# GpSimd's sums for the product M, the attention dots, and layer 3's statistics: three moves in a four-layer graph kernel on one core

## The chip, the core and the metric

The kernel runs on one core of a Trainium2 chip. Five engines of the core work side by side: TensorE (PE; its weight loads are shown as PEld) multiplies matrices into PSUM, VectorE (DVE), ScalarE (ACT) and GpSimd (POOL) work element by element, and SyncE (SP) starts transfers. Each engine takes its instructions strictly in the order in which the program emits them, and waits on semaphores for the others. The metric is the device time of one execution in microseconds (us); lower is better.

## The reference

x is 128 x 128 x 512 (batch, nodes, features), adj is 128 x 128, all float32. Four layers follow one another, and each ends in a normalization over the 512 features:

```python
x = layernorm(x + ((adj @ x) @ W0 + bias0))
q, k, v = x @ Wq.T, x @ Wk.T, x @ Wv.T
rel = adj.T * (q @ k.T);  rel = rel / norm(rel, axis=2)
x = layernorm(x + rel @ v)
h = x @ W;  e = leaky_relu(h@a1[:, None] + h@a2[None, :]) * adj
x = layernorm(x + elu(softmax(e) @ h + beta * h))
A = adj @ x;  C = A + b
x = layernorm(x + max(relu(A + (C - A)), over the last axis))
```

In layer 3 the sum A + (C - A) has the largest element of a row of A, plus b: a row gets relu(max(A row) + b) added to every element.

## The kernel before

The 128 batch elements are worked in 32 groups of four (G = 4). A group passes the four layers; several groups are in flight at once.

**Products.** Four products of a group use a seven-multiplication scheme for 2 x 2 blocks (names y, m, v, z; PSUM tiles r_y, r_m, r_v, r_z). Their left factors need four sums of blocks, which GpSimd builds (`left_factors`, lines 294 to 311: s_y, s_x, s_z; the sums for M and V are the s_x made by `x_sums`). A product has seven steps in the order 1, 2, 6, 5, 7, 3, 4; each step's result is taken from PSUM by ScalarE (a copy) or VectorE (an addition) 0.72 after the step (`product`, lines 339 to 362). Steps 1, 6, 7 and 4 share one PSUM region, so step 7's result must have been taken before step 4 begins, and y's step 6 needs step 1's taken. M's step 6 needs the second sum, step 5 the first, step 7 the third, step 3 the fourth.

**Order.** Nothing is ordered by a planner at run time. Every piece of work is given a time in slots (`TABLE`, lines 231 to 246; 28 slots a group, about 2.4 us each), all pieces are sorted by it and emitted in that order (line 783), which fixes each engine's queue. `FIRST` and `LAST` hold other times for the first two and the last three groups; in `LAST` they are in us, divided by 2.48. The times within a group run over 108 slots, so group g+1's `m` at 28 stands at g's slot 56, and next to it on the queues are g's dots, g+2's `bias` and `y_sums` and g-1's `elu`.

**Around the change.** In layer 1, `residual` (lines 545 to 556) adds rel @ v out of PSUM (p_o) and takes statistics (BATCH_NORM_STATS2 into st, the aggregate into mv). `dots` (lines 559 to 572) multiplies a row block of x2 with two vectors on VectorE and accumulates (tile scr; two per batch element, both inputs in SBUF); `scale_dots` (lines 574 to 587) turns the sums d into layer 2's s1 and s2 in three tiny operations; `spread` transposes them (p_s). `norm` (lines 375 to 406) makes 1/sqrt(variance) with a GpSimd power (ve into rstd), then nmean on VectorE and one ScalarE ACTIVATE per batch element. `elu` (lines 716 to 724) has two VectorE operations with both inputs in SBUF (x from c, x from m). `biased` (line 429) adds bias0 on GpSimd once p_y has been read from x. Layer 3 (lines 747 to 771): `widen` computes adj @ x into p_a, `top` takes the row maximum (mx), adds b and clips (top, VectorE), and ScalarE adds top to x; then statistics and `norm` as in the other layers.

Of the kernel before, what the change touches and what calls it, by code (L numbers as in the profile page):

```python
# [8 lines left out]
FP = mybir.dt.float32  # L9
AF = mybir.ActivationFunctionType  # L10
ALU = mybir.AluOpType
AX = mybir.AxisListType

EPS = 1e-5
# [15 lines left out]
def kernel(  # L30
# [33 lines left out]
    pe, dve, act, pool = (InOrder(tc, e) for e in (nc.tensor, nc.vector, nc.scalar, nc.gpsimd))  # L64
    sync = InOrder(tc, nc.sync)
    B, N, D = x.shape
    P = 128
# [4 lines left out]
    G = 4  # L72
# [5 lines left out]
    work = ctx.enter_context(tc.tile_pool(name="work", bufs=1))  # L78
    small = ctx.enter_context(tc.tile_pool(name="small", bufs=4))
    psum = ctx.enter_context(tc.tile_pool(name="psum", bufs=4, space=bass.MemoryType.PSUM))  # L80

    def bank(name):
        return psum.tile([P, D], FP, tag="ps", name=name)
# [8 lines left out]
    x1, x2, x3 = {}, {}, {}  # L92
# [28 lines left out]
    b3_sb = const.tile([P, 1], FP)  # L121
# [4 lines left out]
    mhalf = const.tile([P, G], FP)  # L126
# [93 lines left out]
    def emit(at, f, *args):  # L220
        pieces.append((at, lambda: f(*args)))

    def each(at, f):
        for b in range(len(at)):
            emit(at[b], f, b)

    def row(at, step, n=G):
        return [at + i * step for i in range(n)]


    TABLE = dict(
        load=[-20], y=row(0.5, 1), bias=row(1.3, 1), y_sums=row(5.2, 0.5), y_w=row(7, 1, 7),
        stats0=row(14.4, 0.4), norm0=[16.2], apply0=row(16.8, 0.33),
        turn=row(21.4, 1), turn_blocks=row(18.4, 0.6),
        move=row(20.5, 0.1), x_sums=row(25.3, 0.5), m=row(28, 1, 7), scores=row(36.5, 1),
        masked=[39.95], squares=[40.4], turn_rel=[40.3],
        move_rel=row(41.2, 0.1), inverse=[42.5], v=row(42, 1, 7), attend=row(50.6, 1),
        residual=row(51.0, 1), dots=row(54.2, 1.1), norm1=[55.2], scale=[58.8],
        apply1=row(65.4, 0.33),
        spread=[61.6], leaky=[62.0], weighted=[63.4], greatest=[64.3], exps=[64.4],  # L240
        divide=[65.8], turn_att=[68.6], with_beta=[69.0], gather=row(71.5, 1),
# [2 lines left out]
        widen=[98.7, 100.0, 103.6, 104.6], top=[99.1, 100.4, 104.0, 105.0],  # L244
        stats3=[99.8, 101.1, 104.7, 105.7], norm3=[106.2], apply3=row(107, 0.33), store=[108.5],
# [8 lines left out]
            stats3=[27.0, 29.9, 32.2, 35.8], norm3=[42.0], apply3=row(44.0, 0.8), store=[47.4],  # L254
        ),
        NG - 2: dict(
            scale=[5.6], apply1=row(24.3, 0.8), spread=[6.9], leaky=[7.4], weighted=[9.0],
# [4 lines left out]
            top=[73.7, 74.6, 78.0, 78.9], stats3=row(79.8, 0.9), norm3=[83.4],  # L262
            apply3=row(84.8, 0.8), store=[88.2],
        ),
        NG - 1: dict(
            m=[0.0, 1.73, 3.46, 5.2, 7.4, 9.1, 10.8], scores=row(12.7, 0.9), masked=[16.4],
            squares=[17.2], turn_rel=[17.1], move_rel=row(18.0, 0.1), inverse=[20.0], v=[16.7, 18.4, 21.0, 22.7, 25.3, 27.9, 30.5],
            attend=row(33.2, 0.86), residual=row(34.1, 1.65), norm1=[40.65], dots=row(40.7, 1.53),
            scale=[47.0], apply1=row(47.5, 0.8), spread=[48.9], leaky=[49.4], weighted=[51.0],
# [5 lines left out]
            top=[83.5, 84.4, 85.3, 87.0], stats3=[86.1, 87.9, 88.8, 89.7],  # L275
            norm3=[86.9, 88.7, 89.6, 90.5], apply3=[88.3, 90.1, 91.0, 91.9],
# [91 lines left out]
    def stats(s, g, b, t):  # L368
        if b == 0:
            s["mv"] = small.tile([P, G, 2], FP, tag="mv", name=f"mv_{g}", bufs=6)  # L370
        st = small.tile([P, 6], FP, tag="st", name=f"st_{g}_{b}")
        dve.bn_stats(st, t)
        dve.bn_aggr(s["mv"][:, b, :], st)

    def norm(at, apply_at, s, g, t):

        n = G // len(at)

        def spread(i):
            sl = slice(i * n, i * n + n)  # L380
            ve = small.tile([P, n], FP, tag=f"ve{n}", name=f"ve_{g}_{i}")
            dve.tensor_scalar(ve, s["mv"][:, sl, 1], EPS, None, op0=ALU.add)
            s["r", i] = small.tile([P, n], FP, tag=f"rstd{n}", name=f"rstd_{g}_{i}")
            pool.tensor_tensor(s["r", i], ve, mhalf[:, sl], ALU.pow)

        def shift(i):
            sl = slice(i * n, i * n + n)
            s["nm", i] = small.tile([P, n], FP, tag=f"nmean{n}", name=f"nmean_{g}_{i}")
            dve.scalar_tensor_tensor(
                s["nm", i], s["mv"][:, sl, 0], -1.0, s["r", i], op0=ALU.mult, op1=ALU.mult  # L390
            )

        def apply(b):
            i, j = b // n, b % n
            act.activation(
                t()[:, b, :],
                t()[:, b, :],
                AF.Identity,
                bias=s["nm", i][:, j : j + 1],
                scale=s["r", i][:, j : j + 1],  # L400
            )

        each(at, spread)
        for i in range(len(at)):
            emit(apply_at[i * n] - 0.1, shift, i)
        each(apply_at, apply)
# [340 lines left out]
    def layer3(g, t):  # L747
        s = {}

        def widen(b):  # L750
            s["a", b] = bank(f"p_a_{g}_{b}")
            pe.matmul(s["a", b], adjT, x3[g][:, b, :], start=True, stop=True)

        def top(b):
            x = x3[g][:, b, :]
            mx = small.tile([P, 1], FP, tag="mx", name=f"mx_{g}_{b}")
            dve.tensor_reduce(mx, s["a", b], AX.X, ALU.max)
            tp = small.tile([P, 1], FP, tag="top", name=f"top_{g}_{b}")
            dve.tensor_scalar(tp, mx, b3_sb, 0.0, op0=ALU.add, op1=ALU.max)
            act.activation(x, x, AF.Identity, bias=tp)  # L760

        def store(i):
            for b in range(i * n, i * n + n):
                sync.dma_start(out[g * G + b], x3[g][:, b, :])

        n = G // len(t["store"])
        each(t["widen"], widen)
        each(t["top"], top)
        each(t["stats3"], lambda b: stats(s, f"3_{g}", b, x3[g][:, b, :]))
        norm(t["norm3"], t["apply3"], s, f"3_{g}", lambda: x3[g])  # L770
        each(t["store"], store)


# [6 lines left out]
    for g in range(NG):  # L780
        for layer in (layer0, layer1, layer2, layer3):
            layer(g, times(g))
# [31 lines left out]
```

## Time and profile before

| | |
|---|---|
| time, median of three | 2234.3 us (2232.62 to 2236.04) |
| span of the profiled execution | 2234.4 us |
| TensorE, weight loads | 2182.9 us busy (98%), 1842.1 us (82%) |
| VectorE, ScalarE, GpSimd | 1794.9 us (80%), 980.0 us (44%), 983.1 us (44%) |
| dots (scr from x and wa), 256 of them | 286.2 us, 1169 ns each |
| statistics, 512 | 352.1 us, 688 ns each; aggregates 93.3 us |
| sums for M (s_x), 128 | 195.1 us |
| Relu-like top on VectorE, 128 | 27.5 us, 215 ns each |

The profile is one execution. A group line has the engine, the operation, output and inputs by the program's names (numbers left out), and how often it ran. The timeline has start and length in us, engine, line, operation, tiles, shapes, and in brackets how long the engine had stood idle and for whom. Line 26 is the helper through which every instruction goes, so groups are told apart by their tiles.

### The profile page before, as it was taken

How to read it: one execution, taken by the hardware profiler on the slowest of the kernel's cores; microseconds unless marked ns; L12 is line 12 of the kernel's file. 1: busy time of each engine (PE TensorE's matmuls, PEld its weight loads, DVE VectorE, ACT ScalarE, POOL GpSimd, SP SyncE). 2: the span in 40 equal slices, each digit the busy share in tenths (PEclk: the TensorE clock that was granted, in tenths of full speed). 3: DMA queues.
4: the chain of work that ended last, by engine and by line, in shares of the span. 5: the costliest groups of instructions: out<-in, count | busy, mean ns of one | idle time of the engine just before them, and what ended most of it. 6: DMA issues, size and time to landing. Idle time of an engine off the chain costs nothing.

```text
span 2234.4 us, 31661 instructions
## 1 busy us (share of the span) xinstructions
PE 2182.9 (98%) x11073; PEld 1842.1 (82%) x11073; DVE 1794.9 (80%) x3534; ACT 980.0 (44%) x1936; POOL 983.1 (44%) x743
## 2 busy tenths in 40 slices
PE   7999999999999999999999999999999999999996
PEld 5888888888888888888888888888888888888873
DVE  4668888778878788888788888788888788887788
ACT  2224444444444454444444444444344444444535
POOL 3435454435455344544344554344553354443322
PEclk9999999999999999999999999999999999999998
DMA  4010222211222211222201222202222112221101
GB/s 166 25 32 19 60 57 62 62 28 40 60 59 62 62 19 48 59 60 62 59 19 52 58 61 62 52 22 55 57 62 63 41 28 59 58 62 43 21 28 57
DMA packets 333294, 115.15 MB, mean 52 GB/s; under 512 B 297424, under 2 KB 297552, under 8 KB 333136
## 3 DMA queue, kind: packets, MB, share of 16 engines
q1 hardware_dynamic: 331936, 110.77, 19.6%
q10 hardware_dynamic: 1200, 2.36, 0.3%
q8 instruction: 89, 1.46, 0.3%
q14 instruction: 69, 0.57, 0.1%
HBM read 39.65 MB, written 33.55 MB: 33 GB/s over the span
## 4 chain that ended last, share of the span: by engine, by line
PE 75%; DVE 20%; issue 3%; POOL 1%; ACT 1%; DMA 0%; DVEq 0%; ACTq 0%; POOLq 0%
PE r_v L26 17%; PE r_y L26 15%; PE r_z L26 14%; PE r_m L26 8%; DVE scr L26 6%; DVE x L26 6%; PE p_z L26 5%; PE p_o L26 5%; PE p_a L26 5%; PE p_rel L26 4%; DVE st L26 2%; PE p_y L26 2%; DVE tT L26 1%; DVE d L26 1%; PE p_m L26 1%
## 5 line engine op out<-in xcount | busy, mean ns | idle before, releaser
L26 ACT ACTIVATE x<-x,nmean,rstd 128x512 f32<-128x512 f32 x512 | 385.8, 808 | 187.5 <-DVE nmean L26 187.4
L26 DVE BATCH_NORM_STATS2 st<-x 128x6 f32<-128x512 f32 x512 | 352.1, 688 | 56.7 <-ACT x L26 47.9
L26 DVE SCALAR_TENSOR_TENSOR scr<-x,wa 128x512 f32<-128x512 f32 x256 | 286.2, 1169 | 0.0
L26 POOL TENSOR_TENSOR rstd<-ve,mhalf 128x4 f32<-128x4 f32 (+1 forms) x134 | 145.2, 1083 | 286.9 <-DVE ve L26 280.7
L26 POOL TENSOR_TENSOR x<-x,bias_sb 128x512 f32<-128x512 f32 x128 | 193.2, 1519 | 76.9 <-PE p_y L26 76.4
L26 POOL TENSOR_TENSOR s_x<-xT 128x512 f32<-128x512 f32 x64 | 95.8, 1497 | 256.5 <-DMA xT<-xB 237.6
L26 ACT ACTIVATE x<-x,top 128x512 f32<-128x512 f32 x128 | 92.4, 722 | 229.1 <-DVE top L26 228.8
L26 DVE TENSOR_TENSOR x<-r_y,x 128x512 f32<-128x512 f32 x224 | 151.4, 676 | 27.1 <-PE r_y L26 27.0
L26 ACT COPY c<-r_z 128x512 f32<-128x512 f32 x124 | 71.8, 579 | 221.5 <-PE r_z L26 221.5
L26 ACT COPY yT<-p_y 128x512 f32<-128x512 f32 x128 | 75.1, 587 | 206.5 <-PE p_y L26 206.5
L26 PEld LDWEIGHTS p_y<-adjT,x 128*128 128x128 f32 x1024 | 135.8, 195 | 13.1 <-ACT adjT L26 5.2
L26 DVE SCALAR_TENSOR_TENSOR x<-p_o,rn,x 128x512 f32<-128x512 f32 x128 | 95.9, 749 | 59.9 <-PE p_o L26 56.0
L26 PE MATMUL p_y<-adjT,x 128*128 128x128 f32 x1024 | 136.7, 278 | 6.4 <-ACT adjT L26 4.9
L26 PEld LDWEIGHTS p_z<-eT,x 128*128 128x128 f32 x1024 | 133.9, 192 | 8.4 <-DVE x L26 1.2
L26 DVE SCALAR_TENSOR_TENSOR x<-m,x 128x512 f32<-128x512 f32 x128 | 129.7, 1013 | 13.6 <-DVE x L26 0.9
L26 PEld LDWEIGHTS p_rel<-xT,tT 128*128 128x128 f32 x1024 | 134.1, 191 | 7.4 <-DVE tT L26 0.8
L26 POOL TENSOR_TENSOR s_z<-zT 128x512 f32<-128x512 f32 x31 | 39.3, 1267 | 224.0 <-ACT zT L26 224.0
L26 PE MATMUL p_rel<-xT,tT 128*128 128x128 f32 x1024 | 134.9, 275 | 0.6 <-DVE tT L26 0.6
L26 PE MATMUL p_z<-eT,x 128*128 128x128 f32 x1024 | 134.8, 275 | 0.4 <-DVE x L26 0.4
L26 PE MATMUL p_a<-x,adjT 128*128 128x512 f32 x256 | 131.2, 597 | 3.6 <-ACT x L26 1.9
L26 ACT COPY tT<-r_m 128x512 f32<-128x512 f32 x128 | 75.7, 591 | 132.9 <-PE r_m L26 132.9
L26 PE MATMUL p_o<-v,relT 128*128 128x512 f32 x256 | 130.3, 593 | 0.0
(119 smaller groups left out, 5008.6 us busy)
## 6 DMA issues: line engine op xcount, KB each, us to landing
out_dram<-x SPq DMA_DIRECT2D x128, 256.0 KB, 2.5
x<-in_x_dram SPq DMA_DIRECT2D x31, 1024.0 KB, 5.8
xT<-xB SPq DMA_DIRECT2D x480, 64.0 KB, 2.3
relT<-relB SPq DMA_DIRECT2D x512, 16.0 KB, 1.8
w_sb<-in_L_gnn_weight_dram ACTq DMA_DIRECT2D x1, 1024.0 KB, 5.9
x<-in_x_dram SPq DMA_DIRECT2D x4, 256.0 KB, 7.9
wq_sb<-in_L_gnn_Wq_dram SPq DMA_DIRECT2D x1, 1024.0 KB, 12.1
wk_sb<-in_L_gnn_Wk_dram SPq DMA_DIRECT2D x1, 1024.0 KB, 14.9
```

The source lines that it names most:

```text
L26: return lambda *args, **kw: self.tc.keep_in_program_order(op(*args, **kw))
```

## The change

Three things change. The four sums for M, which stood 2.7 to 1.2 slots before M's first step, are put at its beginning (27.95, 28.6, 30.0, 31.0, with M at 28), the bias additions 0.3 later. The dots, which stood 1.1 apart from 54.2 on, are put at 51.7, 53.8, 54.9 and 55.6, between and right after the residuals, with norm1 at 54.6 instead of 55.2 and the scaling of the dots at 57.2 instead of 58.8; they are meant to run where GpSimd is quiet. And layer 3 no longer takes statistics on VectorE: ScalarE squares x and accumulates the sum of squares before `top`, the addition of top accumulates the sum, and the variance is made of both; top itself becomes a ScalarE Relu with b as its bias. The times in `FIRST` and `LAST` stay.

```diff
-        load=[-20], y=row(0.5, 1), bias=row(1.3, 1), y_sums=row(5.2, 0.5), y_w=row(7, 1, 7),
+        load=[-20], y=row(0.5, 1), bias=row(1.6, 1), y_sums=row(5.2, 0.5), y_w=row(7, 1, 7),
...
-        move=row(20.5, 0.1), x_sums=row(25.3, 0.5), m=row(28, 1, 7), scores=row(36.5, 1),
+        move=row(20.5, 0.1), x_sums=[27.95, 28.6, 30.0, 31.0], m=row(28, 1, 7), scores=row(36.5, 1),
...
-        residual=row(51.0, 1), dots=row(54.2, 1.1), norm1=[55.2], scale=[58.8],
+        residual=row(51.0, 1), dots=[51.7, 53.8, 54.9, 55.6], norm1=[54.6], scale=[57.2],
...
+        def squares(b):
...
+            act.activation(scr, x3[g][:, b, :], AF.Square, accum_out=s["sq"][:, b : b + 1])
...
-            tp = small.tile([P, 1], FP, tag="top", name=f"top_{g}_{b}")
-            dve.tensor_scalar(tp, mx, b3_sb, 0.0, op0=ALU.add, op1=ALU.max)
-            act.activation(x, x, AF.Identity, bias=tp)
+            tp = s["top"][:, b : b + 1]
+            act.activation(tp, mx, AF.Relu, bias=b3_sb)
+            act.activation(x, x, AF.Identity, bias=tp, accum_out=s["sum"][:, b : b + 1])
+
+        def spread(i):
...
+            dve.tensor_scalar(s["mean", i], s["sum"][:, sl], -1.0 / D, None, op0=ALU.mult)
+            d = small.tile([P, n], FP, tag=f"l3_d{n}", name=f"d3_{g}_{i}")
+            dve.tensor_tensor(d, s["mean", i], s["top"][:, sl], ALU.add)
+            dve.scalar_tensor_tensor(d, d, -1.0, d, op0=ALU.mult, op1=ALU.mult)
+            dve.tensor_scalar(s["sq"][:, sl], s["sq"][:, sl], 1.0 / D, EPS, op0=ALU.mult, op1=ALU.add)
+            dve.tensor_tensor(d, d, s["sq"][:, sl], ALU.add)
+            pool.tensor_tensor(s["r"][:, sl], d, mhalf[:, sl], ALU.pow)
+
+        def shift(i):
...
+            dve.tensor_tensor(s["mean", i], s["mean", i], s["r"][:, sl], ALU.mult)
...
         each(t["widen"], widen)
+        for b in range(G):
+            emit(t["widen"][b] - 0.1, squares, b)
         each(t["top"], top)
-        each(t["stats3"], lambda b: stats(s, f"3_{g}", b, x3[g][:, b, :]))
-        norm(t["norm3"], t["apply3"], s, f"3_{g}", lambda: x3[g])
+        each(t["norm3"], spread)
+        for i in range(len(t["norm3"])):
+            emit(t["apply3"][i * n] - 0.1, shift, i)
+        each(t["apply3"], apply)
```

More of the change, by code (lines that the diff above doesn't have):

```diff
@@ L752, in widen @@
             pe.matmul(s["a", b], adjT, x3[g][:, b, :], start=True, stop=True)
+        def squares(b):
+            if b == 0:
+                for key in ("sq", "sum", "top", "r"):
+                    s[key] = small.tile([P, G], FP, tag=f"l3_{key}", name=f"{key}_{g}", bufs=2)
+            scr = work.tile([P, D], FP, tag="scr3", name=f"scr3_{g}_{b}")
+            act.activation(scr, x3[g][:, b, :], AF.Square, accum_out=s["sq"][:, b : b + 1])
         def top(b):
@@ L757, in top, with apply @@
             dve.tensor_reduce(mx, s["a", b], AX.X, ALU.max)
-            tp = small.tile([P, 1], FP, tag="top", name=f"top_{g}_{b}")
-            dve.tensor_scalar(tp, mx, b3_sb, 0.0, op0=ALU.add, op1=ALU.max)
-            act.activation(x, x, AF.Identity, bias=tp)
+            tp = s["top"][:, b : b + 1]
+            act.activation(tp, mx, AF.Relu, bias=b3_sb)
+            act.activation(x, x, AF.Identity, bias=tp, accum_out=s["sum"][:, b : b + 1])
+        def spread(i):
+            sl = slice(i * n, i * n + n)
+            s["mean", i] = small.tile([P, n], FP, tag=f"l3_mean{n}", name=f"mean3_{g}_{i}")
+            dve.tensor_scalar(s["mean", i], s["sum"][:, sl], -1.0 / D, None, op0=ALU.mult)
[6 more added lines that the diff above has]
+        def shift(i):
+            sl = slice(i * n, i * n + n)
+            dve.tensor_tensor(s["mean", i], s["mean", i], s["r"][:, sl], ALU.mult)
+        def apply(b):
+            x = x3[g][:, b, :]
+            act.activation(
+                x,
+                x,
+                AF.Identity,
+                bias=s["mean", b // n][:, b % n : b % n + 1],
+                scale=s["r"][:, b : b + 1],
+            )
         def store(i):
```

## The prediction

> **What bounds the kernel now.** I read the page first: engine sums and chain.
>
> ```profile
> PE 2182.9 (98%) x11073; PEld 1842.1 (82%) x11073; DVE 1794.9 (80%) x3534; ACT 980.0 (44%) x1936; POOL 983.1 (44%) x743
> ...
> PE 75%; DVE 20%; issue 3%; POOL 1%; ACT 1%; DMA 0%; DVEq 0%; ACTq 0%; POOLq 0%
> ```
>
> TensorE carries the end, yet 20% of the chain runs through VectorE. So I took the window sums of two neighbouring groups (length, then PE, PEld, DVE, ACT and POOL busy, clock, DMA):
>
> ```profile
> 1042.44:1111.74 69.30, 67.75 (x346) 57.35 (x345) 57.48 (x110) 30.35 (x60) 31.34 (x23) 1.00 0.20 50
> 1111.74:1178.55 66.81, 66.81 (x346) 57.16 (x344) 54.63 (x110) 30.34 (x60) 30.50 (x23) 1.00 0.21 52
> ```
>
> The same work takes 66.81 or 69.30 us. By matmul spacing in the timeline, 224 x 0.2158 (256 wide) + 96 x 0.111 + 16 x 0.431 + 8 x 0.11 = 66.8 us is TensorE's floor. Groups 2 to 29 average 67.57 us (from the fourth p_o at 233.07 to that at 2125.06, 28 groups), so 0.76 us a group, 21 us in all, is stall. The timeline names it:
>
> ```profile
> 1062.13 1.99 PE L26 MATMUL r_m<-xT,t_m 128*128 128x256 f32 x8 [1.28 <-DVE tT L26]
> ...
> 1068.71 1.97 PE L26 MATMUL r_y<-t,s_y 128*128 128x256 f32 x8 [0.24 <-DVE x L26]
> ```
>
> TensorE waits for VectorE's additions out of PSUM. VectorE is late because of one thing, seen in the timeline of VectorE and GpSimd:
>
> ```profile
> 1119.22 0.68 DVE L26 SCALAR_TENSOR_TENSOR scr<-x,wa 128x512 f32<-128x512 f32 x1
> ...
> 1119.53 1.50 POOL L26 TENSOR_TENSOR x<-x,bias_sb 128x512 f32<-128x512 f32 x1
> ...
> 1119.83 1.75 DVE L26 SCALAR_TENSOR_TENSOR scr<-x,wa 128x512 f32<-128x512 f32 x1
> ...
> 111.66 1.72 POOL L26 TENSOR_TENSOR x<-x,bias_sb 128x512 f32<-128x512 f32 x1
> ...
> 112.78 1.84 DVE L26 SCALAR_TENSOR_TENSOR d<-mv,wa_sum,d 128x4 f32<-128x4 f32 x2
> 113.33 1.26 POOL L26 TENSOR_TENSOR s_y<-yT 128x512 f32<-128x512 f32 x1
> 114.67 1.26 POOL L26 TENSOR_TENSOR s_y<-s_y,yT 128x512 f32<-128x512 f32 x1
> 114.72 1.23 DVE L26 TENSOR_TENSOR d<-d,rstd 128x8 f32<-128x8 f32 x1
> ```
>
> A dot is 0.68 us beside a quiet GpSimd and 1.75 beside a working one; even a four-element operation waits out a whole GpSimd one (1.23 us instead of 0.17).
>
> **The Trainium skill.** "SBUF — State Buffer", section "Who interferes with whom", says that a VectorE instruction with two SBUF inputs and a GpSimd instruction that reads SBUF exclude each other for the whole instruction, whichever starts first, while one SBUF input does not contend. The trace agrees: a PSUM addition beside a bias addition stays at 0.68. Prices used: "ScalarE: Activation LUTs", section "What ACT_TABLE_LOAD costs" (ACTIVATE 186 ns + 0.833 per element, about 93 more per pointer operand); same page, "Table sets: the hidden batching unit": Relu is in every set. The one table load of the trace (1283 ns) should stay one.
>
> **The change, part by part.** Times below are in us from b, the start of the second half of a group's fourth p_o (1111.74 in the window above).
>
> *Layer 3.* VectorE loses four BATCH_NORM_STATS2 (0.69), aggregates (0.10 more each) and the top (0.13 in the queue): 3.7 us a group. It gains four small operations over the one before, about 0.8 us. That is in a stretch (b-30 to b-8) where its timeline has waits of 1.2 and 1.9 us and no TensorE wait points at it: worth nothing in the steady part. ScalarE gains four Squares, not in the trace at this width: 0.295 for 128 elements plus 384 x 0.833 = 0.615 (the page's price gives 0.613), four 1-column Relus (0.19 to 0.28 by the page; I take 0.28), and 0.09 per accumulator read: 4 us on 30.34 of 66.81. The Squares stand ahead of v's first copy (needed 3 us later) and in idle ScalarE time before tops 2 and 3; behind them the first copy of z ends at b-9.0 for a matmul at b-7.3. The new wait, VectorE for ScalarE's sum, ends near b-9.4; the pow ends by b-7.5, and behind it stands the first residual, which waits for its p_o until b-7.13 anyway. Nothing.
>
> *Dots 0 and 1 move up.* VectorE idles 0.9 us before each of residuals 1 and 2. Dot pair 0 (2 x 0.61) goes from b-5.5 to b-4.3, pair 1 from b+0.44 to b+1.66, both with GpSimd quiet. Residual 3 starts at R = b+1.66 instead of +0.63.
>
> *GpSimd.* norm1's pow (54.6) now precedes the s_x sums (55.95 on), so they no longer start when xT lands (b+0.2 to +1.7) but after ve and pow; behind the waiting pow stand the s_x, bias and y sums, and TensorE's r_m and r_y steps wait for those. In the rows of before, mv starts 1.51 after a residual, pow 0.466 after mv, lasts 1.017, and the next operation starts 0.02 before its end: s_x1 starts R + 2.97 = b+4.64. VectorE: ve 0.217 after mv, addition c 0.075 later, first dot of pair 2 0.605 later, the second 0.61 later: b+4.68. GpSimd is first by about 0.04 us. In the rows of before, whichever starts some 0.01 us earlier gets through. From there the two alternate, at 1.69 per pair of full operations (VectorE's next starts 0.49 after a GpSimd end; GpSimd ends 1.14 after a VectorE end):
>
> s_x1 to 5.91, dot to 6.46; s_x2 to 7.60, dot to 8.15; bias0 to 9.29, dot to 9.84; s_x3 to 10.98; scale, now early, meets GpSimd at full work, and its three tiny operations each wait one out: s_x3 10.98, bias1 12.22, s_x4 13.46. The tT addition then ends at 14.1. First elu: bias2 until 14.69, its first operation to 15.24, bias3 to 16.38, its second to 16.92; statistics; tT addition of step 7 ends 18.46. Step 4 of r_m would start at 18.25 and starts 0.06 after that addition: stall 0.27. Second elu against the y sums: 19.41, 19.96, 21.10, 21.64; statistics; third tT addition ends 23.18. Before, r_y's third step started 2.07 after that end (22.66 to 24.73): 25.25 against an unstalled 24.33. Before, groups with 22.64 to 22.90 here took 0.94 to 1.4 over the floor, some 0.5 beyond that step's delay. So 0.92 + 0.5 = 1.4 us a group, every group.
>
> So the dots themselves finish 2.3 to 3.4 us earlier than before (b+9.8 against 12.0 to 13.2), but GpSimd's queue is pushed 3 to 4 us later and loses the pauses (waits for p_y of 1.0 and 1.3 us) in which scale and the first elu ran free. M's own needs are met: s_x2 at 7.60 for a step at 9.12, s_x4 at 13.46 for 16.09.
>
> Sum, steady part: 28 x (1.4 - 0.76) = +18. Group 1, now 2.9 over the floor: -1.5.
>
> *Start.* In group 0 M begins at b+0.43, as no z product stands between; s_x2, then ready near b+10.4, is needed at 5.7: +4.8; the 2.2 wait of p_s for d there falls away: +2.5.
>
> *End.* The p_s wait (1.14) and the p_rel wait (0.78) of the last M go: -1.9. The removed statistics let the last group's residuals start 1 to 2 us earlier: -1.5. But in the last stretch ScalarE is nearly full:
>
> ```profile
> 2206.98:2231.31 24.33, 11.68 (x24) 4.22 (x22) 21.20 (x62) 18.00 (x26) 5.35 (x9) 0.75 0.17 63
> ```
>
> It has 6.3 us free and gets eight Squares (4.9), eight Relus (2.2) and reads (0.7): 7.8, of which I put 3 on the end, since VectorE loses some 4.6 at the same time (8 x 0.92 less five times 0.55, my estimate for the longer chain of small operations at each of five norms). Together -0.5, uncertain by 4.
>
> 2234.3 + 18 - 1.5 + 2.5 - 0.5 = 2253.
>
> **Rivals.** *A: the lock falls the other way* (the second dot of pair 2 starts first, or the chain is shorter by 1 us). One dot more runs free; the tT addition of step 7 ends at 17.4, the third at 22.0, below the 22.26 from which r_y's step is late. Then all stalls go: 2234.3 - 21.2 - 2.9 + 2.5 - 0.5 = 2212. For it: the margin is 0.04 us and the durations are sums of many rows. Against: the rows are steady to 0.01 us. *B: stalls as large as before:* delays come out half a microsecond smaller than I make them, about 2234. *C: worse:* the sums for M also stall TensorE, or ScalarE sets the last stretch: a further 0.5 us a group and 5 at the end, about 2272.
>
> **Numbers.** My case 0.57, A 0.30, B 0.06, C 0.07. My case with stalls of 0.9 to 1.9 a group gives 2239 to 2267. A reaches from 2206 to 2218. Range 2208 to 2266: some 0.07 of A and nearly all of C fall outside it, with a little of my case. Slower 0.60, the same 0.06, faster 0.34.
>
> **What would show it.** Right: periods of one length near 68.2; r_m's last step waiting 0.2 to 0.4 for tT and r_y's third for x in every group; three of eight dots at 1.75; d at 1.2 us in every group; s_x starting 3 us after residual 3 starts; a new wait of r_m for s_x near 105 us. Wrong: 66.81 periods with the second dot of pair 2 at 0.68 (A); table loads above one, or TensorE waiting for ScalarE's copies (layer 3 not free).

## The result and the profile after

The changed kernel takes 2258.91 us (2258.18 to 2259.69), beside 2235.17 us (2232.62 to 2237.45) for the kernel before on the same chip: 1.0107 times as long, 95% interval 1.0089 to 1.0124. It is slower by 1.1%; 2253 us had been predicted.

The page of the changed kernel, engine sums and chain of waits (the two lines that answer to the first two shown of before):

```profile
PE 2200.1 (97%) x11073; PEld 1846.6 (82%) x11073; DVE 1742.2 (77%) x3290; ACT 1100.8 (49%) x2448; POOL 964.4 (43%) x743
...
PE 62%; DVE 31%; issue 3%; ACT 2%; POOL 1%; DMA 0%; DVEq 0%; ACTq 0%; POOLq 0%
```

VectorE is busy 53 us less in all, and still its share of the chain rose from 20% to 31%. It has less to do and is waited for more. The window sums of two neighbouring groups after (length, then PE, PEld, DVE, ACT, POOL busy, clock, DMA):

```profile
985.78:1053.93 68.15, 67.74 (x345) 57.35 (x344) 54.08 (x102) 34.11 (x76) 30.20 (x23) 1.00 0.21 52
1053.93:1122.10 68.17, 67.75 (x346) 57.36 (x345) 54.10 (x102) 34.12 (x76) 30.21 (x23) 1.00 0.21 51
```

Where the 28 groups of before took 66.81 to 69.37 us, now 27 of them take 68.15 to 68.18 and one 68.46: one pattern, repeated, with the same stall each time. ScalarE has 3.8 us more a group (4 had been expected). TensorE's timeline in the group that starts at b = 1053.93 has the two largest places of the stall, and the last one:

```profile
1072.36 1.99 PE L26 MATMUL r_m<-xT,t_m 128*128 128x256 f32 x8
...
1079.06 1.97 PE L26 MATMUL r_y<-t,s_y 128*128 128x256 f32 x8 [0.36 <-DVE x L26]
...
1089.53 1.59 PEld L26 LDWEIGHTS r_y<-t,yT 128*128 128x128 f32 x8 [0.28 <-DVE x L26]
```

r_m's last step starts at b+18.43 instead of 18.25, and r_y's third at b+25.13 instead of 24.33; the second carries a wait for VectorE in its brackets. Set beside an unstalled group, matmul by matmul, the delay grows by 0.28 us at the first place and by 0.60 at the second. Two later steps of r_y add 0.17 and 0.31; the weight load of the last of them waits 0.28 us for VectorE. That makes 1.36 in all. Why VectorE is late is in the timeline of VectorE and GpSimd:

```profile
1058.01 0.68 DVE L26 SCALAR_TENSOR_TENSOR scr<-x,wa 128x512 f32<-128x512 f32 x1
1058.55 1.26 POOL L26 TENSOR_TENSOR s_x<-xT 128x512 f32<-128x512 f32 x1
...
1058.62 1.75 DVE L26 SCALAR_TENSOR_TENSOR scr<-x,wa 128x512 f32<-128x512 f32 x1
...
1063.66 2.44 DVE L26 SCALAR_TENSOR_TENSOR d<-mv,wa_sum,d 128x4 f32<-128x4 f32 x2
1064.81 1.26 POOL L26 TENSOR_TENSOR x<-x,bias_sb 128x512 f32<-128x512 f32 x1
1066.04 1.27 POOL L26 TENSOR_TENSOR s_x<-xT,s_x 128x512 f32<-128x512 f32 x1
1066.20 1.13 DVE L26 TENSOR_TENSOR d<-d,rstd 128x8 f32<-128x8 f32 x1
1067.26 0.68 DVE L26 TENSOR_TENSOR tT<-r_m,tT 128x512 f32<-128x512 f32 x1
1067.27 2.96 POOL L26 TENSOR_TENSOR x<-x,bias_sb 128x512 f32<-128x512 f32 x2
1067.86 1.24 DVE L26 SCALAR_TENSOR_TENSOR x<-c,x 128x512 f32<-128x512 f32 x1
```

The first sum for M starts 0.07 us ahead of the second dot of pair 2, and from there the two engines take turns. Three dots take 1.75 us. The three small operations of scale (d; the first two share a line) end only with a GpSimd operation each and take 3.7 us together, from b+9.73 to b+13.40. The tT addition stands behind them, and behind it the first elu operation (x from c) meets the next bias addition.

All the time that the kernel lost can be placed. From the spans, with b of groups 2 and 30 as marks, the start (to b of group 2) grew from 233.1 to 235.7 us, the 28 groups between from 1892.0 to 1908.8, and the end from 109.3 to 112.2: 2.6 + 16.8 + 2.9 = 22.3 us, which is 2256.7 less 2234.4. The end is where the prediction missed. Window sums of the last stretch after, of the same kind as the last fence of the prediction, from the corresponding ScalarE instruction to 2.9 us before the end:

```profile
2226.38:2253.80 27.42, 12.63 (x24) 4.40 (x22) 16.17 (x58) 25.78 (x58) 5.35 (x9) 0.70 0.15 58
```

ScalarE is busy in 25.78 of 27.42 us there, 94%; VectorE has become the emptier of the two. The timeline of that stretch shows the queue:

```profile
2237.36 0.61 ACT L26 ACTIVATE scr<-x 128x512 f32<-128x512 f32 x1
2237.51 2.05 PE L26 MATMUL p_a<-x,adjT 128*128 128x512 f32 x2 [2.62 <-ACT x L26]
...
2240.52 0.61 ACT L26 ACTIVATE scr<-x 128x512 f32<-128x512 f32 x1
...
2242.16 0.80 ACT L26 ACTIVATE x<-x,nmean,rstd 128x512 f32<-128x512 f32 x1
...
2243.01 2.08 PE L26 MATMUL p_a<-x,adjT 128*128 128x512 f32 x2 [3.45 <-ACT x L26]
```

The last p_a of the kernel waits for the last ACTIVATE of layer 2's normalization (x from x, nmean, rstd), and that stands behind four Squares (scr from x; the first and the last are shown), two Relus and two additions of top in ScalarE's queue. From the first ACTIVATE with nmean of this stretch to the end of the span the changed kernel takes 30.35 us (from 2226.38) and the kernel before 27.42 (from 2206.98). These 2.93 us are the whole growth of the end. Ahead of that mark both take 81.9 us from b of group 30, but not because nothing changed there: the first experiment shows three differences that cancel.

### The profile page after: what moved, and what is told of

It reads as the page before. It is cut to its first block, busy times and chain, and to the rows that moved or that the text cites. A ratio compares the mean times of both kernels' runs of the same rounds, so it can differ in the third digit from the quotient of the medians.

```text
span 2256.7 us, 31893 instructions
## 1 busy us (share of the span) xinstructions
PE 2200.1 (97%) x11073; PEld 1846.6 (82%) x11073; DVE 1742.2 (77%) x3290; ACT 1100.8 (49%) x2448; POOL 964.4 (43%) x743
## 4 chain that ended last, share of the span: by engine, by line
PE 62%; DVE 31%; issue 3%; ACT 2%; POOL 1%; DMA 0%; DVEq 0%; ACTq 0%; POOLq 0%
PE r_v L26 16%; PE r_y L26 13%; PE r_z L26 12%; DVE x L26 9%; DVE scr L26 9%; PE p_z L26 5%; PE p_a L26 5%; PE p_rel L26 4%; PE p_o L26 4%; DVE d L26 3%; DVE st L26 3%; DVE tT L26 3%; DVE c L26 2%; PE r_m L26 1%; ACT x L26 1%
## 5 line engine op out<-in xcount | busy, mean ns | idle before, releaser
L26 ACT ACTIVATE x<-x,nmean,rstd 128x512 f32<-128x512 f32 x384 | 288.7, 808 | 121.6 <-DVE nmean L26 121.6
L26 POOL TENSOR_TENSOR rstd<-ve,mhalf 128x4 f32<-128x4 f32 (+1 forms) x99 | 98.5, 995 | 528.9 <-DVE ve L26 514.6
L26 DVE BATCH_NORM_STATS2 st<-x 128x6 f32<-128x512 f32 x384 | 263.5, 686 | 8.8
L26 DVE SCALAR_TENSOR_TENSOR scr<-x,wa 128x512 f32<-128x512 f32 x256 | 261.8, 1068 | 0.0
L26 POOL TENSOR_TENSOR x<-x,bias_sb 128x512 f32<-128x512 f32 x128 | 188.4, 1474 | 24.7 <-PE p_y L26 24.6
L26 DVE STREAM_TRANSPOSE xB<-x 128x512 f32<-128x512 f32 x120 | 81.2, 696 | 105.4 <-ACT x L26 84.2
L26 DVE SCALAR_TENSOR_TENSOR x<-m,x 128x512 f32<-128x512 f32 x128 | 140.0, 1094 | 13.2 <-DVE x L26 0.5
L26 DVE TENSOR_REDUCE mx<-p_a 128x1 f32<-128x512 f32 x128 | 87.2, 684 | 57.0 <-PE p_a L26 57.0
L26 DVE TENSOR_TENSOR v<-r_v,v 128x512 f32<-128x512 f32 x96 | 65.8, 686 | 83.9 <-PE r_v L26 78.4
```

Source lines behind the costliest of these rows:

```text
L26: return lambda *args, **kw: self.tc.keep_in_program_order(op(*args, **kw))
```

## The experiments

My theory after the result was the prediction's own: the late sums and the lock between VectorE and GpSimd make the steady loss, and layer 3 costs only at the end. Rivals were that the early dots themselves do harm, by delaying residual 3, and that layer 3's work on ScalarE costs in every group. The table has all kernels that ran; "per group" is the mean over the 28 groups from b of group 2 to b of group 30 in the profiled run, "start" is b of group 2, "end" what follows b of group 30.

| kernel | us | before, beside it | ratio (95%) | start | per group | end |
|---|---|---|---|---|---|---|
| before | | | | 233.1 | 67.57 | 109.3 |
| the change | 2258.9 | 2235.2 | 1.0107 (1.0089 to 1.0124) | 235.7 | 68.17 | 112.2 |
| both table edits, old layer 3 | 2256.0 | 2236.4 | 1.0089 (1.0074 to 1.0104) | 236.2 | 68.19 | 108.3 |
| new layer 3 alone | 2240.1 | 2236.4 | 1.0013 (1.0004 to 1.0023) | 229.9 | 67.56 | 111.7 |
| early dots, norm1, scale alone | 2217.1 | 2236.4 | 0.9917 (0.9902 to 0.9931) | 228.4 | 67.02 | 109.1 |
| late sums and bias alone | 2263.6 | 2236.4 | 1.0122 (1.0105 to 1.0138) | 233.8 | 68.49 | 109.6 |
| the change, norm1 at 54.8 | 2227.3 | 2239.4 | 0.9944 (0.9927 to 0.9961) | 234.9 | 67.07 | 112.9 |
| the change, norm1 at 55.0 | 2241.8 | 2239.4 | 1.0009 (0.9998 to 1.0019) | 237.1 | 67.51 | 112.0 |
| the change without bias additions | 2214.6 | 2239.4 | 0.9889 (0.985 to 0.9929) | 230.4 | 66.83 | 110.6 |
| norm1 at 54.8, old layer 3, early sums in group 1 | 2219.3 | 2235.7 | 0.9921 (0.9909 to 0.9933) | 230.8 | 67.08 | 109.1 |
| the change, scale at 58.8 | 2224.0 | 2235.7 | 0.9945 (0.9932 to 0.9958) | 235.3 | 66.97 | 111.7 |
| two sums early, two late | 2244.9 | 2235.7 | 1.0034 (1.0021 to 1.0047) | 228.4 | 68.07 | 109.3 |
| scale at 58.8, old layer 3, early sums in group 1 | 2218.8 | 2235.6 | 0.9922 (0.9907 to 0.9936) | 229.1 | 67.11 | 108.3 |
| early dots and norm1 alone | 2211.5 | 2235.6 | 0.9888 (0.9872 to 0.9905) | 230.2 | 66.85 | 107.6 |

The last three columns are of one execution each. "Start" and "end" also hold TensorE's granted clock: in ten of the fourteen traces a stretch of 3.3 to 7.2 us at half the clock lies in group 0, and in five (the change, norm1 at 54.8, the change with scale at 58.8, two sums early, and early dots, norm1, scale alone) one of 3.0 to 3.7 us lies in the last group's p_z steps. By the matmul spacings such a stretch makes the column an estimated 1.6 to 2.4 us longer, and no run here shows why it falls where it does. So a difference of that size in one of these two columns is not by itself the edit's.

### The parts of the change, one at a time

**Both table edits with the old layer 3.** The kernel before with the following edit (here and below, only those entries of a table line that differ are shown):

```diff
-bias=row(1.3, 1), x_sums=row(25.3, 0.5),
+bias=row(1.6, 1), x_sums=[27.95, 28.6, 30.0, 31.0],
-dots=row(54.2, 1.1), norm1=[55.2], scale=[58.8],
+dots=[51.7, 53.8, 54.9, 55.6], norm1=[54.6], scale=[57.2],
```

> The kernel before with both table edits (sums for M and bias late; dots, norm1 and scale early) and layer 3 as it was. My theory: the whole steady loss comes from these edits, so every group stays near 68.16 us as in the changed kernel; the +2.8 us at the end came from layer 3 and turns into about -1.9 (the waits of the last M are gone). 2252 to 2255 us where before is 2235. Rival (layer 3's work on ScalarE costs something in every group): groups shorter than 68.16, 2248 or less. Second rival (the end got longer because of the tables): 2258 to 2259.

2256.0 us, 68.19 a group: the steady loss is all there without layer 3. The end is 108.3 us, 3.9 less than with the new layer 3 and 1.0 less than before, where I had expected 1.9 less. In its timeline the last ACTIVATE with nmean follows the first of the same stretch by 11.9 us (2226.45 to 2238.37), in the changed kernel by 15.8 (2226.38 to 2242.16), and the last p_a waits for it 1.43 us instead of 3.45:

```profile
2238.37 0.80 ACT L26 ACTIVATE x<-x,nmean,rstd 128x512 f32<-128x512 f32 x1
...
2239.22 2.08 PE L26 MATMUL p_a<-x,adjT 128*128 128x512 f32 x2 [1.43 <-ACT x L26]
```

From the first of these ACTIVATEs to the end it takes 27.42 us, to 0.01 us what the kernel before takes. So 2.93 of the 3.9 us are the new layer 3 in the last stretch. The rest lies ahead of it, in two parts. With the new layer 3 the last group's p_s starts 0.6 us earlier after its first p_o (19.33 instead of 19.93). And from p_s to the last zT copy it takes 19.16 us instead of 17.60. The reason is TensorE's clock: the window sums from the second p_eT of the last group (the changed kernel first, then this one) have a granted clock of 0.52 and 1.00, and in the timeline eight matmuls of p_z take 1.92 us and 1.06.

```profile
2210.31:2213.81 3.50, 3.50 (x17) 3.50 (x18) 1.19 (x5) 0.59 (x1) 0.00 (x0) 0.52 0.00 0
2211.98:2215.48 3.50, 3.50 (x23) 2.78 (x24) 2.32 (x8) 1.70 (x3) 0.00 (x0) 1.00 0.00 0
```

So beside the kernel before, the changed one gains 1.0 us by the tables and 0.6 by the earlier p_s, and loses 1.6 by the clock and 2.9 in the last stretch.

**The new layer 3 alone.** The changed kernel with the table of before:

```diff
-bias=row(1.6, 1), x_sums=[27.95, 28.6, 30.0, 31.0],
+bias=row(1.3, 1), x_sums=row(25.3, 0.5),
-dots=[51.7, 53.8, 54.9, 55.6], norm1=[54.6], scale=[57.2],
+dots=row(54.2, 1.1), norm1=[55.2], scale=[58.8],
```

> The changed kernel with the old times for sums, bias, dots, norm1 and scale: layer 3's change alone. My theory: groups as before (67.57 on average, a mix of 66.81 and longer ones), only the last stretch longer by 3 to 4.7 us: 2238 to 2240. Rival (layer 3 on ScalarE delays the copies or the residuals in every group): 0.3 us a group or more, 2246 or above. Other side of the rival (VectorE's relief shortens the stalls of before): 2230 or less.

67.56 a group against 67.57, and an end 2.4 us longer: nothing in the steady part, a small loss at the end, and no gain in the groups, although VectorE is busy 3.6 us less in each (51.07 us instead of 54.63 in groups without a stall). From the first ACTIVATE of layer 2's normalization in the last stretch to the end it takes 30.35 us, as the changed kernel does. In all it is slower by 0.04% to 0.23%. The profiled execution took 2235.0 us, 5.1 less than the median of this kernel, so the agreement to 0.01 us a group says little; the 68.17 and 68.19 with and without the new layer 3 say more, since there nearly all groups are equal. The rival that layer 3 costs in every group is out.

**The early dots, norm1 and scale alone.** The kernel before with

```diff
-dots=row(54.2, 1.1), norm1=[55.2], scale=[58.8],
+dots=[51.7, 53.8, 54.9, 55.6], norm1=[54.6], scale=[57.2],
```

> The kernel before with only dots, norm1 and scale moved; sums for M, bias and layer 3 as they were. My theory: the sums for M stand ahead of the pow again and run during the residuals, so most dots run free and no TensorE stall remains: periods near 66.81, 2210 to 2216. Rival (moving the dots up, which delays residual 3 and the statistics behind it, is itself the fault): stalls of 0.8 us or more a group, 2235 or above.

2217.1 us, faster than before by 0.8%. The rival that moving the dots up is itself the fault is out. The expected 66.81 did not come in every group: six of the 28 have some 67.8.

**The late sums and bias additions alone.** The kernel before with

```diff
-bias=row(1.3, 1), x_sums=row(25.3, 0.5),
+bias=row(1.6, 1), x_sums=[27.95, 28.6, 30.0, 31.0],
```

> The kernel before with only the sums for M and the bias additions moved; dots, norm1, scale and layer 3 as they were. My theory: the late sums lock against six or more of the dots, and the delay adds up: about 3.5 us of stall a group, near 2311 (2280 to 2330). Rival (late sums alone are harmless, it is their meeting with the early pow and scale that costs): 68.2 us a group or less, 2258 or below.

2263.6 us, between the two expectations, and the worst kernel of all. Late sums cost 25.8 us over the 28 groups, which is (68.49 - 67.57) x 28. That is 1.7 us of stall a group and not 3.5: three dots are locked (each waits out a GpSimd operation), as in the changed kernel, and not six. So the sums alone account for more than the whole steady loss, and the early dots for a gain of 15.4. But together, with the old layer 3, they give +17.4 and not +10.4, so the parts act on one another.

This kernel also shows how narrow such a meeting can be. Timeline of VectorE and GpSimd in two of its groups, the first elu operation and the bias addition that starts with it:

```profile
1069.69 1.83 DVE L26 SCALAR_TENSOR_TENSOR x<-c,x 128x512 f32<-128x512 f32 x1
1069.71 2.94 POOL L26 TENSOR_TENSOR x<-x,bias_sb 128x512 f32<-128x512 f32 x2
...
1139.09 0.68 DVE L26 SCALAR_TENSOR_TENSOR x<-c,x 128x512 f32<-128x512 f32 x1
1139.10 3.47 POOL L26 TENSOR_TENSOR x<-x,bias_sb 128x512 f32<-128x512 f32 x2
```

VectorE is recorded ahead by 0.01 to 0.02 us in both; in one it gets through, in the other it waits. 22 of the 28 groups go the short way and take about 68.2 us, six go the long way and take 69.4. One lost meeting costs the group 1.2 us.

### Which meeting matters

**norm1 at 54.8.** In the changed kernel VectorE makes ve, for which GpSimd's pow waits, one dot later.

```diff
-norm1=[54.6], scale=[57.2],
+norm1=[54.8], scale=[57.2],
```

> The changed kernel with norm1 at 54.8 instead of 54.6: on VectorE the variance for the pow (ve) stands behind the first dot of pair 2, so GpSimd's pow and first sum s_x1 come some 0.6 us later and one more dot is through before they start. My theory (who starts first at the 0.04 us race of s_x1 and the second dot of pair 2 decides the whole chain): two dots above 1 us instead of three, step 7's addition ends near b+17.2 instead of 18.4, r_y's stalls vanish, periods 66.8 to 67.0: 2216 to 2224 us. Rival (the order at this one place does not matter, GpSimd's total load in this stretch does): 2250 to 2260.

One dot of eight is locked instead of three, step 7's addition ends at b+17.05, and the wait at r_y's third step is gone: 67.07 a group, 31 us less over 28 groups. That is near to what the rival called A in the prediction would have been, though s_x1 now starts 0.82 us later (b+5.44) and two more dots run free, not one. The time, 2227.3 us, is a little above what was expected, since 0.26 us over the floor remains: r_y's last step is still late, and its weight load waits 0.22 us for VectorE.

**norm1 at 55.0.** The same edit with 55.0: ve one dot later still.

> The changed kernel with norm1 at 55.0: ve stands behind both dots of pair 2, so the pow and s_x1 come 1.2 us later than in the changed kernel (s_x1 near b+5.8). My theory: at most one or two dots are locked; s_x2 ends near b+8.8 to 9.0 for a step at b+9.1; periods 66.8, 2216 to 2222 us. Rival (the sums for M are then too late and r_m's second step waits for s_x): a stall of 0.5 us or more at that step in every group, 2232 or above.

Now no dot is locked at all. The dots take 166.9 us over the whole run instead of 261.8 (before: 286.2), and VectorE is busy 47.4 us a group instead of 54.1. And the kernel is no faster than before: the wait of which the rival warned is there, with less than its 0.5 us. TensorE's timeline shows it:

```profile
1056.84 1.59 PEld L26 LDWEIGHTS r_m<-s_x,t_m 128*128 128x128 f32 x8 [0.24 <-POOL s_x L26]
```

s_x1 starts at b+6.66, 0.9 later than I had expected: the pow starts at b+5.32 instead of 3.65, and its row is longer (1.38 us instead of 1.01). The weight load of the sum's step then waits 0.24 us for it, and the step comes out 0.32 late. Most of the rest of the 0.69 us over the floor is r_y's last step, which adds 0.31; its weight load waits 0.28 us for VectorE.

**No bias additions.** The changed kernel with bias0 left out of layer 0, so that it computes something else:

```diff
-each(t["bias"], biased)
```

> The changed kernel without GpSimd's four bias additions (bias0 is left out of layer 0, nothing else changes): 5 to 7 us of GpSimd work a group less, in the very stretch of the dots and the scaling. Theory: VectorE is late because it shares time with GpSimd there; the three operations of scale then find at most one sum to wait for, step 7's addition ends near b+16 to 17 and no stall is left: periods 66.8, 2216 to 2224 us. Rival (VectorE is late because of its own order, with scale and dots ahead of the additions): 2250 or above.

66.83 a group: the stall is gone. The dots are exactly as in the changed kernel, with three of them locked and the last ended at b+9.79. So the locked dots alone don't make TensorE wait. It takes what comes after them: scale now finds one GpSimd operation in its way and not three, and the first elu operation meets no bias addition (timeline of VectorE, b = 1032.11):

```profile
1041.83 1.35 DVE L26 SCALAR_TENSOR_TENSOR d<-mv,wa_sum,d 128x4 f32<-128x4 f32 x2
1043.29 0.17 DVE L26 TENSOR_TENSOR d<-d,rstd 128x8 f32<-128x8 f32 x1
1043.39 0.69 DVE L26 TENSOR_TENSOR tT<-r_m,tT 128x512 f32<-128x512 f32 x1
1044.00 0.68 DVE L26 SCALAR_TENSOR_TENSOR x<-c,x 128x512 f32<-128x512 f32 x1
```

**Scale back at 58.8.** This was meant to show that scale's place in VectorE's queue is of no account.

```diff
-scale=[57.2],
+scale=[58.8],
```

> The changed kernel with scale back at 58.8. My theory (VectorE is late by the number of two-input operations that meet GpSimd's row of six operations, not by scale's place in the queue): scale still ends at one of GpSimd's ends near b+13.5, the second step's addition comes out at b+10.4 instead of 14.0, where nobody waits for it, step 7's addition stays near b+18.4, period 68.1 to 68.2: 2255 to 2260 us. Rival (the early scale is the fault, as it adds three waits that were free before): 66.8 to 67.5 a group, 2220 to 2240.

My theory fell here. 66.97 a group instead of 68.17, and 2224.0 us: the early scale is a fault of its own. I had expected the right times for the addition and for scale's end, and had drawn the wrong conclusion from them. VectorE and GpSimd, b = 1039.09:

```profile
1048.29 1.72 POOL L26 TENSOR_TENSOR s_x<-xT 128x512 f32<-128x512 f32 x1
...
1048.81 0.68 DVE L26 TENSOR_TENSOR tT<-r_m,tT 128x512 f32<-128x512 f32 x1
1049.41 1.84 DVE L26 SCALAR_TENSOR_TENSOR d<-mv,wa_sum,d 128x4 f32<-128x4 f32 x2
...
1051.36 1.13 DVE L26 TENSOR_TENSOR d<-d,rstd 128x8 f32<-128x8 f32 x1
1052.41 0.68 DVE L26 SCALAR_TENSOR_TENSOR x<-c,x 128x512 f32<-128x512 f32 x1
```

Scale ends at b+13.4, as in the changed kernel, because it waits for the same GpSimd operations. But the tT addition, which has one input in PSUM, runs its 0.68 us beside GpSimd's third sum, in time that scale would only have waited. So the first elu starts at b+13.32 and not 13.93, gets through ahead of the next bias addition (0.68 instead of 1.24), and step 7's addition ends at b+17.21 and not 18.37. The Trainium skill says it in "SBUF — State Buffer", section "Who interferes with whom": a VectorE instruction with at most one SBUF input, outside VectorE's two-port modes, does not contend with GpSimd. The 0.68 us beside a working GpSimd agrees. What is to be drawn from it is that such an instruction belongs in front of one that will wait, not behind it.

**Early dots and norm1 alone, scale at 58.8.** The same for the kernel with the early sums.

```diff
-residual=row(51.0, 1), dots=row(54.2, 1.1), norm1=[55.2], scale=[58.8],
+residual=row(51.0, 1), dots=[51.7, 53.8, 54.9, 55.6], norm1=[54.6], scale=[58.8],
```

> The kernel before with the early dots and norm1 only; sums, bias, scale and layer 3 as they were. With scale early the same kernel had 67.02 a group, from some groups with a stall of 0.94. Theory (scale behind the addition costs less wherever a bias addition of GpSimd runs at that moment): those groups lose most of their stall, 66.81 to 66.9 on average: 2209 to 2214 us. Rival (scale's place matters only where the sums are late): 67.0, 2216 to 2219. Other side: scale, moved back behind the addition, now meets the next bias addition in groups where it ran free: 67.2 or more, 2221 or above.

2211.5 us, the fastest kernel of all, 1.1% faster than before. One of 28 groups still has a stall, of 1 us. So with early sums the early scale costs (67.02 - 66.85) x 28 = 4.7 us, and with late sums (68.17 - 66.97) x 28 = 33.6. The page of this kernel, engine sums and chain:

```profile
PE 2170.8 (98%) x11073; PEld 1839.4 (83%) x11073; DVE 1788.2 (81%) x3534; ACT 980.5 (44%) x1936; POOL 963.4 (44%) x743
...
PE 93%; DVE 4%; POOL 1%; ACT 1%; issue 1%; DMA 0%; ACTq 0%; DVEq 0%; POOLq 0%
```

VectorE's share of the chain fell to 4%, while its busy time is nearly that of before (1794.9 us), and its dots take 294.9 us, longer than in any other kernel here. Set beside the kernel with norm1 at 55.0, where the dots took 166.9 us, this shows that their speed is not what TensorE waits for.

### Attempts at a better version with late sums

**norm1 at 54.8, the old layer 3, and early sums for group 1 alone.** The kernel with both table edits and the old layer 3, and in it

```diff
-norm1=[54.6],
+norm1=[54.8],
-1: dict(y=row(-9.5, 0.3), bias=row(-9.2, 0.3))
+1: dict(y=row(-9.5, 0.3), bias=row(-9.2, 0.3), x_sums=row(25.3, 0.5))
```

> Late sums with norm1 at 54.8 (as in the run before), the old layer 3, and the four sums early again for group 1 alone. My theory, part by part: steady groups 67.06 (28 of them 1877.7 us); without the late sums of group 1 the start of group 2's interval falls from 234.9 to near 228.5; with the old layer 3 the end is 108.3 instead of 112.2: 2214.5 span, about 2216 us. Rival for the end (it was not layer 3 that made it longer): 2220 us. Rival for the start (the 4.7 us were not the late sums): 2222 or above.

2219.3 us, some 3 above what was expected. The end is 109.1, close to the 108.3 expected; of the 3.8 us less than with the new layer 3, 2.9 are in the last stretch (27.42 us again). The start is 230.8 and not 228.5. The wait of r_m for s_x near 110 us is gone, so group 0 takes 64.1 us, where it took 68.6 in the changed kernel. But this run's first b came 0.4 us later than with both table edits (99.56 instead of 99.13), and one stretch of matmuls at half their rate (0.43 us instead of 0.22), with the granted clock at half, fell into r_y's steps.

**Scale at 58.8 with the same additions.** The last kernel with

```diff
-norm1=[54.8], scale=[57.2],
+norm1=[54.6], scale=[58.8],
```

> Late sums and early dots with scale at 58.8, the old layer 3, and the four sums early for group 1 alone. Theory from the run with scale back: an addition out of PSUM, which does not lock, runs while scale would only have waited, so step 7's addition ends at b+17.2 and the steady groups stay at 66.97 (28 of them 1875 us); with the start of the early sums (228.4 to 230.8 at group 2's b) and the old layer 3's end (108.3) the span is 2212 to 2214.5: 2213 to 2216 us. Rival (the new layer 3 had a part in that gain): 67.2 a group or more, 2220 or above.

2218.8 us, between the two expectations. 67.11 a group on average: 26 groups near 67.0, and two, of 68.17 and 68.55, in which the first elu lost its meeting with the bias addition though it was recorded 0.009 and 0.017 us ahead. In the other 26 it was 0.009 to 0.019 ahead and got through.

**Two sums early and two late.**

```diff
-x_sums=row(25.3, 0.5),
+x_sums=[25.3, 25.8, 30.0, 31.0],
```

Beside it stand the early dots and scale, the bias additions 0.3 later, and early sums for group 1.

> Old layer 3, the early dots, and the first two sums at 25.3 and 25.8 with the last two at 30 and 31 (early for group 1 alone). My theory: the pow waits behind two sums that run during the residuals, then dots 2 and 3 and scale meet GpSimd only at the first bias additions; one or two dots and at most one small operation are locked, no stall in any phase of the transfers: periods 66.8 to 66.9, start as with early sums, end 108 to 109: 2208 to 2213 us. Rival (splitting the sums only moves the meeting to the bias additions): 67.5 a group or more, 2227 or above.

A miss: 68.07 a group and slower than before. Of the 28 groups all with a first sum at b+0.42 or earlier take some 69.3 us or more, and all with one at b+0.44 or later 66.81, but for one at b+0.55; its start is set by the transfer of xT. In the slow groups the first sums lock both dots of pair 1 and residual 3 comes later. Then two or three more dots and scale meet the bias additions and the late sums, so that step 7's addition ends at b+19.64. The split gives two meetings in place of one.

## Why the prediction was right, and where it was not

**Steady part: right.** The stall was put at 1.4 us a group, and 1.36 were measured (68.17 less 66.81). The replay held step by step: residual 3 at b+1.67 (1.66 in the prediction), s_x1 at 4.62 (4.64), the locked dot at 4.69 (4.68), the dots' end at 9.79 (9.84), the first tT addition at 14.0 (14.1), step 7's at 18.37 (18.46), the third at 23.05 (23.18), r_y's third step at 25.13 (25.25). +16.8 us came of the +18, and group 1 gave -1.52 of the -1.5. The 0.5 beyond the delay of r_y's third step, which had been read from groups of before, is there too: 0.17 and 0.31 at the two later steps of r_y.

**The race: it fell as forecast, and how much hangs on the place is shown.** GpSimd's s_x1 came first by 0.07 us in every group. With ve one dot later the sums start later, the chain on VectorE is shorter, and most of the stall goes. That run moves GpSimd's whole row and not the race alone. Rival A's time of 2212 was too low for that case, though: it left out the 0.26 us a group that remain, and it had A's start and end wrong in the same way as mine.

**"Whichever starts some 0.01 us earlier gets through": too sharp.** In the kernel with late sums alone, leads of 0.013 to 0.018 us in the record went both ways.

**Which edit does it: incomplete.** The prediction named the three waits of the early scale, and they came as worked out, but it did not ask what the same work would cost in the old order. I took the late sums behind the pow as the cause. The runs show a product of two: with early dots, late sums and the old scale leave little stall (66.97), and so do early sums and the early scale (67.02); together they make 68.17. The early dots have their part too: late sums and the old scale with the old dots take 68.49.

**Layer 3 free in the steady part: right.** 68.17 against 68.19 with the rest, and 67.56 against 67.57 alone, in one execution. A Square takes 0.62 us in its row (0.615 in the prediction), the one-column Relu 0.29 (0.28), and the table is still loaded once.

**Start: a term was mis-sized.** +2.5 had been put down for group 0; it takes 4.7 us longer, and b of group 0 came 0.6 earlier. r_m's third step, which waits for s_x, starts 5.24 us later than before (4.8 in the prediction), and the 2.24 of p_s for d is gone, but r_y's third step then comes 1.02 us later still, which I had not followed that far. A stretch at half the granted clock lies in group 0 of both kernels (0.57 on average from 116 to 120 us before, 0.54 from 107.5 to 115 after); by the matmul spacings it costs an estimated 1.7 us before and 2.4 after.

**End: two terms were mis-sized and one was missing, and this is 3.4 of the 6 us by which the time was missed.** "Together -0.5" measured +2.9. The term that looked least certain was right: 3 us had been put down for ScalarE, and the last stretch grew by 2.93, in every kernel with the new layer 3 (30.34 or 30.35 us in six traces) beside every kernel with the old one (27.41 to 27.43 in eight). But it came from comparing busy times of ScalarE and VectorE, without a look at ScalarE's queue, so the close fit is in part luck. The timeline has the path: the Squares stand ahead of layer 2's last ACTIVATEs, for which the last p_a of the kernel waits. No run moved the Squares within the queue, so the path is read and not tested. What failed is the rest. The tables gave -1.0 and not -1.9, since the wait of p_rel (0.82) did not go. The residuals did start earlier, the last by 2.4 us, but only 0.6 of the 1.5 put down for it reached p_s: r_z's steps ahead of p_s still wait 1.4 us for GpSimd's s_z and 1.1 for ScalarE's c. And 1.6 us at half the granted clock had no term at all. -1.0 - 0.6 + 1.6 + 2.9 = 2.9. Of the remaining miss 1.6 us are the start's, the steady part came 1.2 short of its +18, and the rest lies between the profiled executions and the medians.

## What to carry to other kernels

Where two engines shut one another out, count the waits in queue order up to the instruction that the bounding engine needs. Do not count the busy time of the locked instructions: the kernel with the fastest dots gained nothing, and the one with the slowest dots was the best. An instruction that cannot be locked out, such as an addition that reads PSUM, belongs ahead of one that will wait (1.2 us a group here). A move of work that costs nothing in the steady part has to be looked at again at the end of the kernel, where the engine that receives it may be the one that is full. And before a term is blamed for a loss, split the loss at marks that all kernels share: here the end as a whole seemed to accuse ScalarE's term, and the split shows that it was the one that came out right.

## What the hardware showed that I had not expected

- In the record, the start of an instruction does not tell who gets through when the two are within about 0.02 us. The Trainium skill, "SBUF — State Buffer", section "Who interferes with whom", says that issue order decides who blocks. At a lead of 0.07 us the changed kernel agrees: s_x1 started first and took 1.26 us, and the dot took 1.75. Below 0.02 us the record cannot say. In the kernel with late sums VectorE's recorded lead was 0.013 to 0.018 us in 22 groups where it took 0.68 us, and 0.000 to 0.018 in six where it took 1.83. In the kernel with scale back at 58.8 all 28 got through with 0.005 to 0.019.
- The lock is not even between small and large. A VectorE operation on four columns waits out a 512-column addition of GpSimd (1.13 us instead of 0.17). But GpSimd's four-column pow did not hold up the dots that ran beside it: with norm1 at 55.0 two dots of 0.68 us each run while the pow is open, and it is the pow whose row is longer, 1.38 us instead of 1.01.
- TensorE's granted clock falls to half for stretches of 3.0 to 7.2 us in group 0 and in the last group's p_z steps, in some traces and not in others; in the end of the changed kernel this cost 1.6 us. Why it does so there isn't shown.
